# A list scheduler runs sixteen turns instead of eight, and chooses the issued pass by its length plus its stretches of thin TensorE work

## The chip, the cores and the metric

The kernel is one program on one core of one Trainium2 chip. The metric is the device time of one execution in microseconds (us). Before the change the median of 9 runs was 2910.94 us, the lowest 2896.37 and the highest 2915.04.

A core has five instruction queues that matter here: TensorE (PE in the profile, its weight loads under PEld), VectorE (DVE), ScalarE (ACT), GpSimd (POOL) and SyncE (SP, which here only issues DMA transfers). Each engine takes its instructions in the order of its own queue, and engines wait for each other through semaphores. So the kernel's time depends on the order in which instructions stand in these queues.

## What is computed

The reference is a decoder of four layers in float32 on 2048 tokens (32 sequences of 64) of width 256, with a second input `ctx` of 2048 rows of width 128. Every layer is an attention (or state-space) part, a cross-attention to `ctx` and a feed-forward part, each behind a layer norm and added to the residual. With the weights left out of the calls it reads:

```python
x = x + _L0_attn_ref(_layernorm(x), ...)    # attention and gated linear attention, 32 heads
x = x + _L0_xattn_ref(_layernorm(x), ctx_1024, mask, ...)   # cross-attention, 16 heads of 128
x = x + _L0_ffn_ref(_layernorm(x), ...)
x = x + _L1_attn_ref(_layernorm(x), ...)    # state-space mixer, 32 heads, scan over time
x = x + _L1_xattn_ref(_layernorm(x), ctx_1024, ...)
x = x + _L1_ffn_ref(_layernorm(x), ...)     # router, 8 experts of 256
x = x + _L2_attn_ref(_layernorm(x), ...)    # chunked state-space mixer
x = x + _L2_xattn_ref(_layernorm(x), ctx_1024, ...)
x = x + _L2_ffn_ref(_layernorm(x), ...)     # binarized linear layer
x = x + _L3_attn_ref(_layernorm(x), ...)    # attention with fake-quantized fp4 linears
x = x + _L3_xattn_ref(_layernorm(x), ctx_1024, pos, pos, ...)
x = x + _L3_ffn_ref(_layernorm(x), ...)     # top 6 of 64 experts, each at most 128 tokens
```

## The kernel before

The 2048 tokens lie as 16 tiles of 128 tokens, and each tile's residual stays in on-chip memory (`X`, named `__init___x` in the profile). The tiles go through the layers in three groups of 8, 6 and 2 tiles (`GROUPS`, L2559). While one group is in the later layers, the next is recorded beside it in the earlier ones, by `weave` (L2594). Only the last group has nothing behind it: `run_last` (L2585) records its late layers beside the 64 experts of layer 3, which serve the tokens of the first two groups.

Nothing is issued while this is recorded. A `Recorder` keeps each instruction as an `Op` with the engines it may run on, its views of tiles, and the later ops that must follow it (`after`). A copy out of PSUM or an elementwise combination may have two possible engines (`either`, `combine`); on which one it runs, and in which of the buffers of its kind (`Net.SLOTS`, L804) a tile lies, is settled by the scheduler.

The scheduler is `Order` (L539). It goes through planned time: `run` (L621) keeps for each of the five engines the ops whose predecessors are planned, and plans next the one that can start earliest. `duration` (L475) gives the length it assumes for an instruction, and `may_open` (L567) keeps an op from taking a buffer that an earlier op needs. An op may be planned ahead of recorded order by at most `horizon` (120) us of TensorE work. Where TensorE would wait for more than 1.6 us (`IDLE`) and a PSUM bank is free, `fill` (L597) plans a matmul of constants whose result nobody reads, once per step, until the wait is used up. These fillers are named `spare_mm` in the profile.

`in_turns` (L785) repeats this. It plans the program forwards, then plans the reversed graph (`backwards`), with ops numbered by their planned starts (`renumber`), then forwards again, and so on. Each plan starts from the starts of the one before. With `rounds` = 4 there are nine passes, of which the first, third, fifth, seventh and ninth go forwards; these five are the candidates. The one with the least planned length is kept, and `issue` (L2517) writes its instructions to the engines' queues in its order. All instructions carry the line of `issue` in the profile (L2541), so they are told apart by the names of their tiles, where the numbers of layers are left out: `L_block_mm` is `L1_block_mm`.

The names that the prediction's steps use:

- `L_block_mm`, `L_block_b`, `L_block_w` (`unit_L1_block`, L1864): one block of 128 queued tokens of layer 1's experts, whose weights are fetched by the block's expert number. Its output is stored to `result` in device memory by SP.
- `L_result_b` (`unit_L1_result`, L1899): GpSimd gathers these rows back per token by indirect DMA (`DMA_INDIRECT`), two gathers per tile, and VectorE adds them to `X`.
- `cross_scores_mm`, `blocks_b`, `cross_out_mm`: the cross-attention of layers 0 and 1: scores on TensorE, softmax on the other engines, then the product with the context.
- `norm_mm`, `norm_sm`, `pair_mm`, `ssm_heads_mm`: a layer norm with its transposition, and the state-space layers.
- `L_experts_mm`, `L_dense_mm`, `L_parts_b`: layer 3's experts for the first two groups; the same experts, computed densely, for the last group's two tiles; and the sum of the experts' parts at the end of the program.

## Time and profile before

| | |
|---|---|
| median of 9 runs | 2910.94 us |
| the profiled execution | 2918.21 us |
| its span, from the first to the last instruction | 2916.4 us |
| mean granted TensorE clock over the span | 0.972 |
| TensorE instructions | 26626 |
| end of the last matmul, from the span's start | 2887.1 us |
| DMA transfers issued by SP | 665 |

The profile is of a single execution, which took 7.3 us longer than the median. Its views give the busy time of each engine, the busy share in slices of time, the chain of work that ended last, the waits of one engine for another, and the instructions in order of time. A float32 matmul runs as two TensorE instructions, a transposition as one, so a count of TensorE instructions in the profile is larger than in the program. A form such as `32*128` ahead of a matmul's shape is the part of the 128 by 128 array that it uses. "PEclk" is the share of full clock that TensorE was granted in a stretch, and "DMA" the mean busy share of the DMA engines.

### The profile page before, as it was taken

To read this page: it belongs to the slowest core of one execution; us is meant where nothing else is said; L and a number is where in the kernel's file an instruction comes from. 1 tells how busy PE (TensorE), PEld (TensorE's weight loads), DVE (VectorE), ACT (ScalarE), POOL (GpSimd) and SP (SyncE) were. 2 spreads that over 40 slices of the span, in tenths; PEclk is the share of its full clock that TensorE was granted. 3 is DMA by queue.
4 is the path that set the end of the run, shared out by engine and by line. 5 is a ranking of instruction groups with operands and counts; after the bars stand their busy time and mean duration, and the time that the engine had idled before them with its cause. 6 is when DMAs were issued, how large, how long until landed. Compare 5 with 4: busy or idle time off the path is not lost.

```text
span 2916.4 us, 66660 instructions
## 1 busy us (share of the span) xinstructions
PE 2811.5 (96%) x26626; PEld 2342.7 (80%) x26626; DVE 2125.1 (73%) x5139; ACT 1518.7 (52%) x2849; POOL 1522.6 (52%) x1304
## 2 busy tenths in 40 slices
PE   8999999999999999999999999999999999998995
PEld 7888888877878788888888778878797878877674
DVE  5664457775767767867688998787846879988853
ACT  5553226665445454544366656666534665376450
POOL 6762232212666645524554437695615477457665
PEclk8999999999999999999999999999899999999977
DMA  4003320400261146122100110022374122211435
GB/s 179 16 13 116 144 104 19 156 2 31 87 253 46 57 160 206 53 65 64 46 20 27 33 56 17 8 96 81 123 263 171 58 72 83 88 50 59 140 115 175
DMA packets 120313, 259.04 MB, mean 89 GB/s; under 512 B 27077, under 2 KB 81880, under 8 KB 107588
## 3 DMA queue, kind: packets, MB, share of 16 engines
q1 hardware_dynamic: 110212, 230.68, 23.0%
q0 software_dynamic: 9792, 24.10, 2.4%
q8 instruction: 211, 3.46, 0.5%
q14 instruction: 98, 0.80, 0.1%
HBM read 179.38 MB, written 78.77 MB: 89 GB/s over the span
## 4 chain that ended last, share of the span: by engine, by line
PE 80%; DVE 10%; ACT 5%; POOL 2%; issue 2%; DMA 1%; SPq 0%; POOLq 0%; ACTq 0%; DVEq 0%
PE L_xattn_mm L2541 13%; PE ssm_heads_mm L2541 10%; PE pair_mm L2541 10%; PE cross_out_mm L2541 9%; PE L_attn_mm L2541 7%; PE L_ffn_mm L2541 5%; PE L_block_mm L2541 3%; PE turn_mm L2541 3%; PE rope_mm L2541 3%; DVE rope_b L2541 2%; PE L_dense_mm L2541 2%; PE cross_scores_mm L2541 2%; ACT rope_b L2541 2%; PE heads_mm L2541 2%; PE norm_mm L2541 1%
## 5 line engine op out<-in xcount | busy, mean ns | idle before, releaser
L2541 PE MATMUL pair_mm<-norm_b,load_ssm_w 128*128 128x256 f32 x1280 | 307.1, 381 | 1.5 <-DVE __init___x L2541 0.5
L2541 PEld LDWEIGHTS pair_mm<-norm_b,load_ssm_w 128*128 128x128 f32 x1280 | 235.0, 190 | 36.8 <-issue 4.6
L2541 POOL TENSOR_TENSOR L_xattn_sm<-L_xattn_sm,__init___consts 128x8 f32<-128x8 f32 (+2 forms) x64 | 190.4, 2982 | 57.9 <-DVE L_xattn_sm L2541 51.1
L2541 DVE SCALAR_TENSOR_TENSOR ssm_heads_b<-pair_mm,load_ssm_wp,ssm_heads_b 128x252 f32<-128x252 f32 (+2 forms) x480 | 197.2, 467 | 22.5 <-ACT ssm_heads_b L2541 21.3
L2541 ACT COPY rope_b<-rope_mm 32x512 f32<-32x512 f32 x234 | 134.7, 577 | 119.0 <-DVE rope_b L2541 71.4
L2541 POOL TENSOR_TENSOR norm_sm<-norm_sm,__init___consts 128x1 f32<-128x1 f32 (+1 forms) x149 | 93.8, 639 | 168.3 <-DVE norm_sm L2541 151.5
L2541 ACT ACT_TABLE_LOAD x136 | 174.5, 1283 | 10.8 <-DVE L_xattn_sm L2541 2.6
L2541 ACT COPY L_xattn_b<-L_xattn_mm 128x512 f32<-128x512 f32 x177 | 103.8, 591 | 130.8 <-PE L_xattn_mm L2541 127.9
L2541 PE MATMUL rope_mm<-norm_b,load_L_attn_w 128*128 128x128 f32 x1280 | 164.1, 283 | 4.3 <-DVE rope_b L2541 2.7
L2541 PEld LDWEIGHTS rope_mm<-norm_b,load_L_attn_w 128*128 128x128 f32 x1280 | 156.4, 198 | 13.7 <-issue 8.8
L2541 PE MATMUL ssm_heads_mm<-load_ssm_w,ssm_heads_b 128*128 128x256 f32 x640 | 160.0, 384 | 0.2 <-DVE ssm_heads_b L2541 0.2
L2541 ACT ACTIVATE ssm_heads_b<-ssm_heads_b 128x512 f32<-128x512 f32 (+1 forms) x152 | 124.4, 833 | 51.8 <-DVE ssm_heads_b L2541 37.0
L2541 POOL TENSOR_TENSOR ssm_heads_b<-ssm_heads_b,ssm_heads_b 128x1024 f32<-128x1024 f32 x33 | 80.6, 2448 | 135.3 <-DVE ssm_heads_b L2541 116.1
L2541 POOL TENSOR_TENSOR rope_b<-rope_b,__init___consts 128x512 f32<-128x512 f32 x72 | 92.9, 1291 | 81.3 <-DVE rope_b L2541 37.2
L2541 PEld LDWEIGHTS ssm_heads_mm<-load_ssm_w,ssm_heads_b 128*128 128x128 f32 x640 | 116.5, 190 | 23.1 <-issue 9.3
L2541 ACT COPY turn_b<-turn_mm 128x512 f32<-128x512 f32 x194 | 106.4, 602 | 52.2 <-PE turn_mm L2541 51.4
L2541 DVE TENSOR_SCALAR norm_b<-__init___x,norm_sm,norm_sm 128x256 f32<-128x256 f32 x192 | 104.9, 565 | 31.2 <-POOL norm_sm L2541 9.4
L2541 PEld LDWEIGHTS L_xattn_mm<-norm_b,load_L_xattn_w 128*128 128x128 f32 x1024 | 121.1, 192 | 7.8 <-issue 5.9
L2541 ACT COPY norm_b<-norm_mm 128x256 f32<-128x256 f32 (+1 forms) x133 | 56.9, 436 | 134.9 <-PE norm_mm L2541 120.4
L2541 POOL TENSOR_TENSOR heads_b<-heads_b,heads_sm 128x1024 f32<-128x1024 f32 x52 | 101.9, 1967 | 46.6 <-DVE heads_sm L2541 26.0
L2541 PE MATMUL L_xattn_mm<-norm_b,load_L_xattn_w 128*128 128x128 f32 x1024 | 125.4, 276 | 0.0
L2541 PE MATMUL cross_out_mm<-load_L_xattn_w,cross_out_b 128*128 128x256 f32 x512 | 123.4, 390 | 0.3 <-ACT cross_out_b L2541 0.2
(439 smaller groups left out, 7893.6 us busy)
## 6 DMA issues: line engine op xcount, KB each, us to landing
L_block_w<-in_f_rows SPq DMA_DIRECT2D x42, 770.0 KB, 6.5
queue<-far_w SPq DMA_DIRECT2D x14, 1024.0 KB, 10.4
load_ssm_w<-in_s_in SPq DMA_DIRECT2D x12, 1024.0 KB, 6.3
parts<-far_w SPq DMA_DIRECT2D x10, 1024.0 KB, 17.0
slots<-far_w SPq DMA_DIRECT2D x16, 548.0 KB, 7.5
L_experts_b<-slots SPq DMA_DIRECT2D x32, 274.0 KB, 5.2
units_L_xattn_w<-kept_x SPq DMA_DIRECT2D x8, 1024.0 KB, 7.9
L_parts_b<-parts SPq DMA_DIRECT2D x14, 512.0 KB, 7.7
```

What stands on the lines that cost most here:

```text
L2541: done = getattr(getattr(nc, e), method)(*map(real, op.args), **kw)
```

## The change

`in_turns` is called with `rounds` = 8, so that there are seventeen passes and nine candidates. The first five are the candidates of before, since nothing in a pass itself has changed. And the candidate that is issued is no longer that with the least planned length, but that with the least sum of planned length and 3.0 us for each thin stretch. `thin` counts these: planned time is cut into stretches of 3.413 us, each instruction of TensorE adds to the stretch in which it starts a weight (for a matmul, its columns times 1.67 ns times the share of the array that it uses; 0.107 us for a transposition; 0.43 us for a filler), and a stretch with less than 0.36 of its length is thin. `Order.run` notes the starts of fillers for it (`fills`).

```diff
@@ -629,6 +629,7 @@
         stuck, done, oldest, result, self.starts = False, [False] * len(self.ops), 0, [], {}
+        self.fills = []
         while not all(done[oldest:]):
@@ -727,7 +728,9 @@
-            if not filler:
+            if filler:
+                self.fills.append(start)
+            else:
                 done[o.at], self.starts[o] = True, (start, len(result))
@@ -782,14 +785,32 @@
+STRETCH, FULL, THIN = 3.413, 0.36, 3.0
+
+
+def thin(plan):
+
+    work = {}
+    for o, (start, _) in plan.starts.items():
+        if o.ways[0][0] == "tensor":
+            k, m = part(o.ways[0][1], o.args)
+            n = o.args[2].size() * 0.00167 * k * m / P**2 if o.ways[0][1] == "matmul" else 0.107
+            at = int(start / STRETCH)
+            work[at] = work.get(at, 0.0) + n
+    for start in plan.fills:
+        work[int(start / STRETCH)] = work.get(int(start / STRETCH), 0.0) + 0.43
+    return sum(work.get(i, 0.0) < FULL * STRETCH for i in range(max(work)))
+
+
 def in_turns(ops, slots, horizon, spare, rounds):
@@
-        if k % 2 == 0 and (best is None or plan.length < best[0]):
-            best = plan.length, result, {t: t.slot for o, _ in result for t in o.tiles}
+        worth = plan.length + THIN * thin(plan)
+        if k % 2 == 0 and (best is None or worth < best[0]):
+            best = worth, result, {t: t.slot for o, _ in result for t in o.tiles}
@@ -2629,7 +2650,7 @@
-    issue(tc, in_turns(net.nc.ops, Net.SLOTS, 120.0, net.spare, 4), Net.SLOTS)
+    issue(tc, in_turns(net.nc.ops, Net.SLOTS, 120.0, net.spare, 8), Net.SLOTS)
```

The program's work is the same in both kernels. What differs is the order in each queue, the buffers, the choice of engine where there are two, and the number of fillers.

## The prediction, on record before the result was known

> **What bounds the kernel now.** I read the page's busy times first, then its clock row and its chain, then the span in forty equal windows, then the waits of TensorE, and last the order of time around the longest run of fillers.

> ```profile
> PE 2811.5 (96%) x26626; PEld 2342.7 (80%) x26626; DVE 2125.1 (73%) x5139; ACT 1518.7 (52%) x2849; POOL 1522.6 (52%) x1304
> PEclk8999999999999999999999999999899999999977
> PE 80%; DVE 10%; ACT 5%; POOL 2%; issue 2%; DMA 1%; SPq 0%; POOLq 0%; ACTq 0%; DVEq 0%
> ```

> TensorE bounds the kernel: busy for 96% of the span, and 80% of the chain that ended last. Its own work is the same in both kernels, so the change can only move three things: time in which TensorE stands idle (2916.4 - 2811.5 = 104.9 us, of which 29.3 lie behind the last matmul, which ends at 2887.1), time in which it runs on a half-rate clock, and fillers. In the windows, the columns behind the busy times are the granted clock, the DMA share and GB/s:

> ```profile
> 876.00:949.00 73.00, 70.98 (x682) 59.63 (x681) 53.10 (x129) 39.46 (x74) 44.24 (x30) 0.95 0.14 48
> 949.00:1022.00 73.00, 66.03 (x676) 56.64 (x675) 57.72 (x157) 33.16 (x67) 45.23 (x39) 0.98 0.17 55
> 1460.00:1533.00 73.00, 69.18 (x670) 58.43 (x669) 59.55 (x149) 51.20 (x93) 39.96 (x35) 0.95 0.06 20
> 2044.00:2117.00 73.00, 70.19 (x616) 55.94 (x616) 59.21 (x170) 35.93 (x69) 48.59 (x41) 0.86 0.39 126
> 2628.00:2701.00 73.00, 63.86 (x683) 50.64 (x680) 61.58 (x192) 42.69 (x91) 56.95 (x53) 0.91 0.20 64
> 2774.00:2847.00 73.00, 70.42 (x645) 53.43 (x644) 40.13 (x130) 36.22 (x75) 47.75 (x48) 0.79 0.33 113
> ```

> The reader is to see that lost clock and lost busy time sit in few places: near 900 to 1170, near 1500, near 2050 and from 2550 on. Clock lost is (1 - clock) x 73 us. Between 73 and 2628 nine windows are below 1.00 (four at 0.95, four at 0.98, one at 0.86): 14.6 + 5.8 + 10.2 = 30.7 us. The three windows from 2628 to 2847 lose 6.6 + 5.1 + 15.3 = 27.0 us, and the first window, at 0.88, 8.8 us.

> ```profile
> PE L_attn_mm L2541 <- DVE rope_b L2541: 8.3, 5, 2.2
> PE L_ffn_mm L2541 <- DVE L_ffn_sm L2541: 4.0, 2, 2.7
> PE ssm_heads_mm L2541 <- DVE ssm_heads_b L2541: 3.6, 3, 3.1
> ```

> No kind of wait is large (columns: total, times, longest). The idle time is many hand-overs from VectorE and ScalarE of 0.3 to 3.1 us. No single wait can be removed for much; a new order redraws them all.

> **The change, part by part.** *Is another order issued?* Yes. The orders of the two programs differ in nearly every run of rows (TensorE's has 5598 rows before and 5403 after). The order issued before is the fifth candidate; now it is the eighth. With each instruction counted at the median interval of its kind in the rows of before, a TensorE instruction stands 4.1 us of TensorE work from its old place on average (median 3.0, one in a hundred over 17). Stages and their sequence stay; neighbours are shuffled.

> *Engines.* 17 copies out of PSUM move from VectorE to ScalarE (0.59 us on ScalarE, 0.69 on VectorE for 128x512), three small products move the other way, three combinations from VectorE to GpSimd, one of 136 table loads (1.28 us) goes. Spread over 2900 us and on engines busy for 52% to 73%, this is hidden beside TensorE; uncovered it would be a few tenths each. I count 0. SP still issues 665 transfers and GpSimd 204 gathers and scatters.

> *Fillers: 42 before, 35 after.* One filler is two passes; 16 of them took 7.07 us, so 0.44 us each. They mark the places where the planner expects TensorE to stand, so their removal is a gain only where real work takes their place. Sixteen of the 42 stand in one place:

> ```profile
> 2187.32 2.08 PE L2541 MATMUL cross_scores_mm<-contextT_cx,L_xattn_b 128*64 128x64 f32 x64
> 2189.33 4.58 PE L2541 MATMUL L_block_mm<-L_block_w,L_block_b 128*128 128x256 f32 x20
> 2193.76 7.07 PE L2541 MATMUL spare_mm<-__init___consts 128*128 128x256 f32 x32
> 2201.89 4.07 PE L2541 MATMUL cross_out_mm<-blocks_b,context_cx 32*128 32x512 f32 x32 [1.06 <-DVE blocks_b L2541]
> ...
> 2219.81 2.75 PE L2541 MATMUL spare_mm<-__init___consts 128*128 128x256 f32 x12
> 2222.47 1.57 PE L2541 MATMUL norm_mm<-__init___consts,norm_b 128*128 128x128 f32 x8
> ```

> Scores end at 2189.4 and the product with the context starts at 2201.9: a softmax of 12.5 us with 4.4 us of expert blocks beside it, and 8.1 us of fillers and wait. In the new order the scores stand ahead of most blocks: between them and the first `cross_out_mm` are 34 block matmuls of 128x128 (16 passes took 1.95 us in a row near 2178, so 68 take 8.3), 4 of 128x256 (8 passes, 1.8), 8 transpositions (0.9) and two fillers (0.9), 11.9 us. That leaves 0.9 of filler and 0.6 of wait: -6.6 us. The blocks' products on GpSimd now fall among the softmax's, but before its weighting GpSimd idled 3.4 us, which takes them.

> What is late next are the blocks' results. Before: last block matmul done at 2193.9, last store issued by SP at 2196.7, first gather on GpSimd at 2208.3, eight gathers to 2218.5, then the norm's power on the same queue, transpositions at 2222.5: 28.6 us. Now ten gathers stand ahead of that power (two more at 1.25 us), so 31.1 us, against 27.7 us of TensorE work between last block and this `norm_mm` (products with the context, six fillers, 27 matmuls of the third group's `L_ffn_mm`, moved forward). TensorE's queue waits 3.4 us there, with `pair_mm` behind it. The place is worth -3.2 us; bounds -6.6 (results in time) and +2 (they come 5 us later).

> *The other fillers.* Between 2640 and 2726, 16 become 21, thirteen of them in one stand ahead of the last two tiles' `L_attn_mm`: +2.2 us. Three new ones in the first 500 us and one less at 2101: +0.9. Each is bounded by the longest wait in the rows: 3.1 us more or 3.1 less per stand.

> *Half-rate clock.* This is what the added term weighs. Row first: the window from 2044 to 2117 has TensorE busy 70.2 of 73 us and yet a clock of 0.86. The work there is on parts of the array (`64*64`, `8*128`, `32*128`), and no wait ahead of the last matmul is over 3.1 us. [...] The nine windows with loss between 73 and 2628 lose 30.7 / 9 = 3.4 us each. How many go, nothing shows: bounds are all nine gone (-30.7) and as many new ones (+30.7). The issued pass is now weighed by them at all, and it displaced the old one, which still is a candidate, so I take two fewer, an estimate: -6.8 us.

> *The end.* Behind the last matmul lie 29.3 us of `L_parts_b` sums. In both orders the last of them is loaded behind the stores of the last two tiles and followed by the same short chain on VectorE and GpSimd: 0 (bounds 2 us either way).

> *Sum:* -3.2 + 2.2 + 0.9 - 6.8 = -6.9 us. The profiled execution of 2918.2 us would become 2911.3; it stood 7.3 above the median, so the median becomes 2904. All other hand-overs are redrawn too: 75.6 us of idle time ahead of the last matmul plus 66.5 of clock. If some forty places of 2 us are redrawn independently, their sum moves by about 2 x sqrt(2 x 40) = 18 us; many are forced by data and stay, so I take two thirds, 12 us.

> **The rivals.** *No change.* The last 260 us are the serial chain of the last two tiles, with VectorE at 18.45 of 20 us between 2640 and 2660 and the lowest clock. If the eighth candidate brings two more half-rate losses there (3.4 each), they pay for the two gone earlier: -6.9 + 6.8, 2911. For it: the end has five more fillers. Against it: these keep TensorE's array full while it waits.

> *Slower, through the gathers.* The gathers are behind the last store, and that shares its queue with 1024 KB weight loads, which took 6.3 to 17.0 us to land. If the first gather starts 17.0 instead of 11.6 us after the last store, TensorE waits 5.4 us more, and a stand of 8.8 us brings a half-rate stretch (3.4); without the gain in thin stretches: -3.2 + 5.4 + 3.4 + 2.2 + 0.9 = +8.7, 2920. It decides from about 2.5 us later than before. For it: a 1024 KB load of `units_L_xattn_w` that was issued 20 us after the last store now stands just ahead of it. Against it: before, three such loads stood there too.

> *Nothing is changed*, because the old pass wins again: the orders exclude it.

> **How the numbers follow.** Forecast (a gain of some us) 46%, its own range 2892 to 2905. No change 20%: within 0.2% (5.8 us, about what a measurement of this kernel can tell from no change), 2905 to 2917. Slower 34%: the gathers, or the redrawn hand-overs coming out badly, which the 12 us allow. Two tenths left out, 2904 with 1.6 times 12 us each way: 2884 to 2924.

> **What would show it.** Right: few fillers near 2190 and `cross_out_mm` less than 2 us after the block matmuls; a mean clock above 0.972, with the window near 2050 above 0.86. Wrong: a wait of over 6 us at `norm_mm` behind `L_result_b`; clock lost in windows that had 1.00; or VectorE's hand-overs from 2550 on grown by ten us or more. The prediction fails most easily where it estimates: in the number of thin stretches, and in the redrawing.

## The result: slower by 1.2%, most of it clock

The changed kernel takes 2945.14 us (median of 15 runs, 2936.3 to 2952.0), the kernel before 2911.78 us (46 runs, 2896.37 to 2924.14): ratio 1.0118, 95% interval 1.0103 to 1.0132, some 33 us. The forecast was 2904, the range 2884 to 2924.

The page after, in the parts that were shown of before (busy times, clock row, chain):

```profile
PE 2819.7 (96%) x26612; PEld 2353.5 (80%) x26612; DVE 2127.6 (72%) x5122; ACT 1518.7 (52%) x2862; POOL 1543.9 (52%) x1307
PEclk8999999999999999999999999999999999999987
PE 76%; DVE 12%; ACT 5%; issue 3%; POOL 3%; DMA 1%; SPq 0%; DVEq 0%; POOLq 0%; ACTq 0%
```

TensorE issues 14 instructions fewer, the fillers that are gone, and yet is busy 8.2 us longer. The other engines are as busy as before, but for 21 us on GpSimd. In the chain TensorE's share falls from 80% to 76%, and VectorE's, GpSimd's and "issue" rise by a point or two each. So neither more work nor a new bottleneck shows here; the same work takes longer.

The windows of after, with the clock behind the busy times:

```profile
584.00:657.00 73.00, 72.03 (x614) 58.47 (x613) 50.10 (x132) 42.95 (x63) 9.37 (x7) 0.95 0.00 1
876.00:949.00 73.00, 69.50 (x661) 56.66 (x654) 44.70 (x110) 34.62 (x67) 38.04 (x27) 0.91 0.17 60
1460.00:1533.00 73.00, 72.03 (x694) 60.96 (x693) 65.24 (x173) 52.28 (x97) 47.00 (x43) 1.00 0.05 17
1825.00:1898.00 73.00, 69.69 (x716) 53.88 (x718) 54.13 (x107) 39.09 (x79) 49.64 (x41) 0.88 0.03 7
2044.00:2117.00 73.00, 67.72 (x613) 56.08 (x612) 64.74 (x164) 34.92 (x69) 55.52 (x48) 0.91 0.36 123
2774.00:2847.00 73.00, 69.34 (x1030) 54.15 (x1018) 58.00 (x210) 48.36 (x106) 47.35 (x49) 0.91 0.49 150
```

Read each against its twin of before, four of which stand in the prediction; the other two are:

```profile
584.00:657.00 73.00, 72.56 (x656) 57.70 (x656) 55.16 (x147) 44.35 (x70) 12.96 (x9) 1.00 0.01 2
1825.00:1898.00 73.00, 70.83 (x791) 57.49 (x790) 58.77 (x147) 46.84 (x91) 48.15 (x41) 1.00 0.04 8
```

The places near 1500 and 2050 that the prediction hoped to mend are mended (0.95 to 1.00, 0.86 to 0.91), and so is the window from 2774 (0.79 to 0.91). But windows that had 1.00 before now lose clock: 584 to 657 (0.95) and 1825 to 1898 (0.88). Set side by side, lost clock seems merely to have moved.

The waits of TensorE (total, times, longest) tell the same story:

```profile
PE turn_mm L2562 <- ACT heads_b L2562: 6.5, 3, 3.8
PE L_attn_mm L2562 <- DVE L_attn_b L2562: 6.4, 3, 3.2
PE L_block_mm L2562 <- DVE L_block_b L2562: 5.1, 4, 2.3
```

Other pairs lead the list than before, and none is large. When the same instructions of the two traces are set against each other, after's lag (the median over the instructions within 25 us) is 13 us by 650, 15 by 1450, back at 3 to 9 from 1500 to 1800, 20 by 1950, 24 by 2450, 34 at 2700 and 24 at 2850: many steps, both ways.

### Where the 33 us are

Two accounts were made. The first goes by the traces up to the last matmul. "Clock" is half of the time at half rate (a granted clock of 0.50; passes of a filler follow each other by 0.216 us at full rate, and by 0.427 in the half-rate stretch of after at 2736.9) in which TensorE worked; "fillers" are their passes at 0.216 us; the rest is TensorE's own work. Both kernels were profiled a second time, under the names `c_before_again` and `c_after_again`:

| execution | last matmul, us from the first | idle | clock | fillers | own work | half-rate stretches |
|---|---|---|---|---|---|---|
| before | 2885.9 | 74.4 | 67.2 | 18.1 | 2726.1 | 19 |
| before, again | 2864.4 | 79.5 | 38.8 | 18.1 | 2728.0 | 13 |
| after | 2910.6 | 90.9 | 77.9 | 15.1 | 2726.7 | 29 |
| after, again | 2909.7 | 93.8 | 76.2 | 15.1 | 2724.5 | 29 |

TensorE's own work agrees within 3.5 us in all four. By the means of each pair, after stands idle 15 us more, loses 24 us more to the clock and spends 3 us less on fillers. From the first execution of each alone, one would have read +16.5 idle and +10.7 clock, and called waits the larger part. That profile of before caught an execution with much half rate: by span and clock it lost 82.9 us, the second one 52.1. The runs of before reach from 55 to 82, so the two stand at its ends, and their mean is near the runs' mean of 67.2 below.

The second account needs no trace. Every run lists its span and mean granted clock, so span x (1 - clock) is the time lost to the clock and span x clock the rest. On one chip, number 12 in the records of the runs:

| kernel | runs | lost to the clock, us | the rest, us |
|---|---|---|---|
| before | 17 | 67.2 | 2840.3 |
| after | 6 | 97.6 | 2846.3 |

The 17 executions of after behind the result, whose chip is not on record, give 97.7 and 2846.1. The clock takes 30 us more, the rest 6 us more. (This counts clock lost while TensorE has nothing to do, too, as in the 25.9 us at half rate behind the last matmul of before: among the runs of before, 1 us lost goes with 0.8 us of span, so by an estimate the 30 are worth about 25.) Both accounts name the clock as the larger part.

### One of the new places

Near 1850 both orders run the cross-attention of small heads. First before, in order of time:

```profile
1860.80 0.61 PE L2541 MATMUL L_xattn_mm<-norm_b,load_L_xattn_w 128*128 128x128 f32 x4
1861.34 2.98 PE L2541 MATMUL heads_mm<-values_b,turn_b 128*64 128x18 f32 x96
1864.25 1.09 PE L2541 MATMUL turn_mm<-__init___consts,heads_b 128*128 128x128 f32 x8
```

Then after:

```profile
1856.30 1.15 PE L2562 MATMUL cross_scores_mm<-L_xattn_b,L_xattn_b 128*64 128x64 f32 x32 [1.35 <-DVE turn_b L2562]
1858.22 1.37 PE L2562 MATMUL turn_mm<-__init___consts,heads_b 128*128 128x128 f32 x8 [0.77 <-ACT keys_apart_b L2562]
1860.14 4.27 PE L2562 MATMUL small_scores_mm<-keys_apart_b,keys_apart_b 32*64 32x256 f32 x32 [0.56 <-DVE heads_sm L2562]
1864.35 5.31 PE L2562 MATMUL heads_mm<-values_b,turn_b 128*64 128x18 f32 x96
```

The clock of the ten microseconds from 1860, before and then after:

```profile
1860.00:1870.00 10.00, 10.00 (x181) 9.48 (x179) 8.18 (x16) 6.68 (x13) 8.99 (x7) 1.00 0.04 10
```

```profile
1860.00:1870.00 10.00, 9.68 (x130) 7.45 (x131) 7.66 (x14) 6.86 (x11) 7.60 (x4) 0.64 0.01 2
```

Before, 96 passes of `heads_mm` (a `128*64` part of the array, 18 columns each) take 2.98 us between products on the full array. After, three waits of 0.6 to 1.4 us come first, and then two thin products stand back to back; the 96 passes take 5.31 us, and 32 passes of `small_scores_mm` take 4.27, which took 1.44 us seven microseconds earlier. The three waits sum to 2.7 us. Half rate begins at 1862.71 only, so the 4.27 us are two things: 24 of the 32 passes start by 1862.12, at full clock, with stands of 0.5 us within them and 0.4 us behind them that the line doesn't show as waits, and the last 1.6 us lie at half rate. The half-rate stretch ends at 1872.95. It is 10.24 us long at a granted clock of 0.50 and costs half of that, 5.1 us, of which 5.31 - 2.98 = 2.3 us are the 96 passes. The second execution of after has a half-rate stretch of 13.7 us at the same place, and the second of before has none there, so it belongs to the order.

### The profile page after: what moved, and what is told of

Read it like the earlier page. It is cut to its first block, busy times and chain, and to the rows that moved or that the text cites. A ratio compares the mean times of both kernels' runs of the same rounds, so it can differ in the third digit from the quotient of the medians.

```text
span 2940.8 us, 66641 instructions
## 1 busy us (share of the span) xinstructions
PE 2819.7 (96%) x26612; PEld 2353.5 (80%) x26612; DVE 2127.6 (72%) x5122; ACT 1518.7 (52%) x2862; POOL 1543.9 (52%) x1307
## 4 chain that ended last, share of the span: by engine, by line
PE 76%; DVE 12%; ACT 5%; issue 3%; POOL 3%; DMA 1%; SPq 0%; DVEq 0%; POOLq 0%; ACTq 0%
PE L_xattn_mm L2562 12%; PE ssm_heads_mm L2562 10%; PE pair_mm L2562 9%; PE cross_out_mm L2562 9%; PE L_attn_mm L2562 7%; PE L_ffn_mm L2562 4%; PE turn_mm L2562 3%; PE rope_mm L2562 2%; PE L_block_mm L2562 2%; PE heads_mm L2562 2%; ACT rope_b L2562 2%; PE L_dense_mm L2562 2%; DVE rope_b L2562 2%; PE cross_scores_mm L2562 2%; PE small_scores_mm L2562 2%
## 5 line engine op out<-in xcount | busy, mean ns | idle before, releaser
L2562 DVE SCALAR_TENSOR_TENSOR ssm_heads_b<-pair_mm,load_ssm_wp,ssm_heads_b 128x252 f32<-128x252 f32 (+2 forms) x480 | 196.2, 467 | 19.2 <-ACT ssm_heads_b L2562 18.1
L2562 POOL TENSOR_TENSOR norm_sm<-norm_sm,__init___consts 128x1 f32<-128x1 f32 (+1 forms) x149 | 93.8, 635 | 172.3 <-DVE norm_sm L2562 157.6
L2562 ACT COPY L_xattn_b<-L_xattn_mm 128x512 f32<-128x512 f32 x167 | 97.5, 587 | 164.5 <-PE L_xattn_mm L2562 152.9
L2562 POOL TENSOR_TENSOR ssm_heads_b<-ssm_heads_b,ssm_heads_b 128x1024 f32<-128x1024 f32 x36 | 87.4, 2428 | 158.2 <-DVE ssm_heads_b L2562 108.2
L2562 POOL TENSOR_TENSOR rope_b<-rope_b,__init___consts 128x512 f32<-128x512 f32 x76 | 102.2, 1346 | 81.0 <-ACT rope_b L2562 51.9
L2562 ACT ACTIVATE ssm_heads_b<-ssm_heads_b 128x1024 f32<-128x1024 f32 (+1 forms) x152 | 124.0, 832 | 37.9 <-DVE ssm_heads_b L2562 16.5
L2562 PE MATMUL L_attn_mm<-load_L_attn_w,L_attn_b 128*128 128x256 f32 x512 | 125.0, 388 | 0.0
L2562 PEld LDWEIGHTS L_xattn_mm<-norm_b,units_L_xattn_w 128*128 128x128 f32 x1024 | 119.8, 192 | 4.3 <-issue 2.3
```

What stands on the lines that cost most here:

```text
L2562: done = getattr(getattr(nc, e), method)(*map(real, op.args), **kw)
```

## The experiments

Eighteen runs follow. The letters in the expectations stand for these theories. A: any redrawn order scatters around a mean, and the fifth candidate, the kernel before, was a good draw. B: more turns pack the plan tighter and leave less room for what the planner doesn't know. C: the planner's own length tells the time. D: its durations for VectorE and GpSimd are too short, and truer ones help. E: the loss is in the choice of engine. T: the planned count of thin stretches tells the real clock. K and W: fillers in waits spare clock, or only trade one loss for another.

By the numbers in the records, chip 12 ran e1 to e4 and the c and n kernels, and chip 11 ran f5 and f6; on both, before takes 2910 to 2911 us, as it does in the result. The other runs came to three other chips (0, 6 and 13), on which before itself takes 3008 to 3011 us; only ratios are compared across chips.

### Other candidates of the same planner

The new length of the search without the new term issues the ninth candidate:

```diff
-    issue(tc, in_turns(net.nc.ops, Net.SLOTS, 120.0, net.spare, 4), Net.SLOTS)
+    issue(tc, in_turns(net.nc.ops, Net.SLOTS, 120.0, net.spare, 8), Net.SLOTS)
```

> Sixteen turns, but the candidate with the least planned length is issued, as before the change: this is the ninth candidate, which the planner puts ahead of all others in length. Theory A (redrawn hand-overs: a candidate's time on the chip scatters by about 1% around a mean that its planned figures do not tell, and the fifth was a low draw): somewhere in 2915 to 2950 us, not the fastest of the candidates. Theory B (each further turn packs the plan closer, with less room at the hand-overs, and costs time on the chip): the slowest of the candidates, 2945 to 2960. Theory C (length tells the time, and the new weighing for thin stretches spoiled the choice): faster than before the change, 2895 to 2908.

Measured: 2924.69 against 2911.38 us, ratio 1.0046 (1.0029 to 1.0064).

The sixth and the seventh candidate are issued by keeping the last pass of five and of six rounds:

```diff
-        if k % 2 == 0 and (best is None or plan.length < best[0]):
+        if k == 2 * rounds:
...
-    issue(tc, in_turns(net.nc.ops, Net.SLOTS, 120.0, net.spare, 4), Net.SLOTS)
+    issue(tc, in_turns(net.nc.ops, Net.SLOTS, 120.0, net.spare, 5), Net.SLOTS)
```

> The sixth candidate is issued, one forward pass after the one issued before the change. By the planner's length it is the worst of the fifth to ninth. Theory A: 2915 to 2950, its place among the candidates not that of its planned length. Theory B: a little slower than the fifth and faster than the seventh, near 2920. Theory C: the slowest of the five, over 2925.

Measured: 2941.26 us, 1.0106 (1.0081 to 1.0131).

> The seventh candidate is issued. By the planner's length it lies just behind the eighth, and far ahead of the sixth. Theory A: 2915 to 2950, no order by planned length. Theory B: between the sixth and the eighth, near 2932. Theory C: faster than the sixth by 6 us or more, and close to the fifth.

Measured: 2922.98 us, 1.0037 (1.0017 to 1.0058).

So the sixth to the ninth candidate stand at 1.0106, 1.0037, 1.0118 and 1.0046: all slower than the fifth, and in no order with the number of turns. B falls. C falls as well: the ninth is the shortest plan and not the fastest. By the planner's own figures and the account of the runs' clocks, all on chip 12:

| candidate | planned length, us | planned thin stretches | lost to the clock, us | the rest, us | ratio |
|---|---|---|---|---|---|
| fifth (before) | 2683.6 | 9 | 69.2 | 2841.5 | 1 |
| sixth | 2691.9 | 11 | 88.2 | 2852.1 | 1.0106 |
| seventh | 2685.7 | 10 | 81.1 | 2840.8 | 1.0037 |
| eighth (after) | 2683.9 | 8 | 97.6 | 2846.3 | 1.0118 |
| ninth | 2678.8 | 10 | 85.9 | 2836.8 | 1.0046 |

By the new score (length plus 3.0 us for each thin stretch) the eighth stands 2.7 us ahead of the fifth and 0.9 ahead of the ninth: against the fifth, a single thin stretch decided the choice.

The new term chose the candidate with the fewest planned thin stretches, and that one loses the most clock of all. The ninth is 5 us better than before in everything but the clock, and loses 17 us there.

### The old engines in the new order

Between the two kernels 643 operations run on another engine (246 from VectorE to ScalarE, 232 back, 84 from VectorE to GpSimd, 81 back). This kernel keeps after's order and buffers, with before's engine for each operation:

```diff
+        if k == 8:
+            old = dict(result)
...
-    return best[1]
+    return [(o, old.get(o, e)) for o, e in best[1]]
```

> The changed kernel's order of all instructions and its buffers, but every instruction that may run on two engines runs on the one that it had before the change (17 copies go back from ScalarE to VectorE, larger products from GpSimd to VectorE). Theory E (the choice of engines costs the time: GpSimd has 21 us more work, 1543.9 against 1522.6, and VectorE's instructions get slower beside it): at least half of the 33 us comes back, 2925 or less. Theory A (the order costs it): the time stays within 10 us of the changed kernel, 2935 to 2955, or is worse, since the order was made for the other engines.

Measured: 3007.47 us, 1.0323 (1.0296 to 1.0350). Its longest waits of TensorE:

```profile
PE turned_mm L2564 <- POOL L_xattn_b L2564: 8.7, 6, 3.8
PE turn_mm L2564 <- ACT heads_b L2564: 7.6, 4, 3.8
PE ssm_heads_mm L2564 <- DVE ssm_heads_b L2564: 7.4, 6, 2.7
```

Putting the engines back costs 62 us more. TensorE now waits for GpSimd and VectorE where the plan had spread the work otherwise; 119 us are lost to the clock. Order and engines are one plan and can't be judged apart in this way. E finds no support. That a VectorE instruction can be slow beside GpSimd the trace of after shows: at 390.92 us a 128x256 scaling into `norm_b` takes 3.69 us beside a 128x2048 product of 3.61 us on GpSimd, where the median of the 192 such scalings is 0.41. What this costs in the new order stays untested.

### Other durations and horizons

The planner was given longer durations for VectorE and GpSimd, nearer to the measured ones, with eight turns and no thin term, and with sixteen and the term:

```diff
-            return 0.16 + n * 0.00052 + 0.11 * small
+            return 0.2 + n * 0.00052 + 0.23 * small
...
-        return 0.15 + n * 0.00104 + 0.06 * small
+        return 0.19 + n * 0.00104 + 0.06 * small
...
-    return 0.14 + n * (0.00174 if full < 2 else 0.0022)
+    return 0.14 + n * (0.00174 if full < 2 and n != 512 else 0.0022)
```

> The kernel before the change, eight turns and choice by length, with the planner's durations for VectorE and GpSimd raised to what the trace of before shows (VectorE 0.04 us more for each instruction and 0.12 more where a small operand goes with a large one in on-chip memory, GpSimd's 512-column products at 1.27 instead of 1.03 us). Theory D (the plan goes wrong on the chip because it has VectorE too fast: 2248 us planned against 2433 measured, so hand-overs that it counts as covered are not): fewer and shorter waits, idle time before the last matmul down from 74 by 20 us or more, time 2880 to 2900. Theory A (any new plan is a new draw, and the draws scatter by 1%): anything from 2900 to 2950.

Measured: 3020.75 against 3007.89 us, 1.0040 (1.0023 to 1.0057).

> The changed kernel, sixteen turns and the choice with thin stretches, with the same raised durations. The planner now counts 14 thin stretches in the candidate that it issues (the seventh) against 22 in the one that the run with eight turns and the same durations issues, at nearly equal planned length. Theory T (the term for thin stretches is right, and it failed only since the planner's times were too short to see the stretches): at least 10 us faster than the run with raised durations and eight turns, and fewer half-rate stretches. Theory A: no relation to that run, within 20 us of it on either side.

Measured: 3065.37 us, 1.0197 (1.0151 to 1.0244).

And the horizon of 120 us was changed by one microsecond each way, which alters nothing but which orders the passes find:

```diff
-    issue(tc, in_turns(net.nc.ops, Net.SLOTS, 120.0, net.spare, 4), Net.SLOTS)
+    issue(tc, in_turns(net.nc.ops, Net.SLOTS, 119.0, net.spare, 4), Net.SLOTS)
```

> The kernel before the change with a horizon of 119 instead of 120 us, which means nothing by itself and gives another family of plans; all of its candidates have a planned length that is longer by about 0.7% than the one issued before. Theory A: 2910 to 2950, a draw like the others. Theory C (planned length tells the time): 2925 to 2940. A time at or below 2911 speaks against both.

Measured: 3015.10 us, 1.0031 (1.0015 to 1.0047).

> The kernel before the change with a horizon of 121 instead of 120 us. Its issued candidate has a planned length that is longer by about 0.6% than the one issued before, and the fewest thin stretches in the planner's count of all plans seen (5, where the kernel before the change has 9 and the changed one 8). Theory T (few planned thin stretches mean few half-rate stretches on the chip): under 15 half-rate stretches and a clock over 0.976, time below 2920. Theory A: 18 to 30 half-rate stretches, 2910 to 2950.

Measured: 3025.67 us, 1.0070 (1.0042 to 1.0097).

D falls: truer durations made the plan no better. T falls for a second time: the plan with a horizon of 121 counts 5 thin stretches, the fewest of all, and loses 127.8 us to the clock, where before with its count of 9 lost 127.7 on that chip; g1's count was 22 and g2's 14, and g2 takes 45 us longer than g1 and loses no less to the clock (148.6 us in four runs that spread from 134 to 163, against 139.5). A holds as far as it goes: all eight other plans, from 1.003 to 1.020, are slower than that of before, and the eighth candidate is not outside their scatter.

### Fillers added, by a rule that was too coarse

Fillers were put ahead of 43 waits of TensorE in before and 48 in after, in any PSUM bank that the order left alone for its next 60 steps (place: number):

```diff
+FILLS = {
+    134: 3, 208: 5, 228: 1, 323: 5, 564: 3, 1120: 5, 1267: 2, 6876: 4, 7161: 2, 7384: 2,
...
+def padded(order, place, spare):
...
-    return best[1]
+    return padded(best[1], place, spare)
```

> The kernel before the change, its order and buffers untouched, with more fillers: 103 filler matmuls are put ahead of the 43 TensorE instructions that had waited for over 0.6 us in the profile of before, as many as fit into each wait. Theory K (half-rate stretches come from windows in which TensorE has too little work, and a wait filled with work on the whole array prevents them): the clock's loss before the last matmul, 67 us, falls by 20 us or more, the fillers lie in time that was idle, and the time falls by 10 to 25 us, 2886 to 2901. Theory W (the clock's loss comes from the work on small parts of the array, not from the waits, or the waits move when they are filled): clock unchanged within 0.003, time 2911 to 2925.

Measured: 3014.44 against 3008.19 us, 1.0028 (1.0011 to 1.0044).

> The changed kernel, its order and buffers untouched, with 144 fillers ahead of the 48 TensorE instructions that had waited for over 0.6 us in its own profile. It has 29 half-rate stretches before the last matmul where before had 19, and 78 us of loss through them where before had 67. Theory K: more is won than in the kernel before, 15 to 35 us, 2910 to 2930, and what remains against the filled kernel before is the difference in waits. Theory W: 2940 to 2960.

Measured: 3036.37 us, 1.0089 (1.0059 to 1.0118).

This could not tell K from W, since most places had no free bank: only 11 further fillers ran in f1 and 21 in f2. Some of them waited for a bank themselves, as f1's waits show (the first line is of another kind, and is met again below):

```profile
PE L_experts_mm L2581 <- issue: 12.0, 24, 1.1
...
PE spare_mm L2581 <- DVE rope_b L2581: 3.7, 1, 3.7
...
PE spare_mm L2581 <- DVE L_attn_b L2581: 3.3, 1, 3.3
```

### Fillers added only where a bank was free

By each kernel's own trace, 15 waits of before and 20 of after had a bank that had been free since before the wait began. They got 36 and 60 fillers (place: number, bank):

```diff
+FILLS = {
+    134: (3, 7), 7161: (2, 0), 7387: (1, 4), 7482: (1, 4), 7860: (2, 5), 11272: (7, 7), 16168: (1, 1), 16666: (3, 6),
+    21392: (2, 0), 22195: (2, 6), 22516: (1, 0), 22601: (2, 7), 22651: (5, 4), 23677: (3, 3), 23682: (1, 5),
+}
...
-    return best[1]
+    return padded(best[1], place, spare)
```

> The kernel before with 36 further filler products, put only ahead of the 15 waits of TensorE for which, by its own trace, a PSUM bank of the filler's kind had been free since before the wait began. Every planned step, engine and buffer is otherwise that of the kernel before. Theory K (idle stretches thin the work, thin work halves the clock, so filling them spares clock): the fillers take the place of waits, the half-rate stretches fall from 19 to 15 or fewer, the clock's cost from 67 us to about 55, and the time falls by 5 to 12 us. Theory W (filling only trades one loss for another: the fillers delay what follows the wait, and other stretches become thin): half-rate stretches 17 or more, time within 0.2% or longer by up to 10 us.

Measured: 2993.92 against 3010.66 us, 0.9940 (0.9924 to 0.9957), faster than the kernel before on that chip. (The counts of stretches in the expectation are those of the first profile of before; here the kernel shows 26.)

> The changed kernel with 60 further filler products, put by the same rule ahead of 20 of its waits. Theory K: half-rate stretches fall from 29 to 23 or fewer, the clock's cost from 78 us to about 60, and the time falls by 8 to 18 us, so that a third to a half of the change's loss is undone without touching the order. Theory W: half-rate stretches 26 or more, the time within 0.2% of the changed kernel's (ratio to before near 1.012) or above it.

Measured: 3025.54 us, 1.0051 (1.0034 to 1.0068).

The changed kernel itself had not been run on that chip, so 1.0051 could not be set against its 1.0118. The two kernels unedited ran on chip 12, and f3's kernel once more, beside one with only the 36, on chip 11:

> The kernel before, unedited, profiled on this chip so that the others of this group have a profile of their own chip beside them. Ratio to itself 1.000; if this chip is the slower one again (before near 3010 us), its waits for the issue of instructions and its clock's cost (above 67 us) show here too.

> The changed kernel, unedited, on the chip of this group. Theory K says that the further fillers (1.0051 with 60 of them) undid part of the loss: then the changed kernel alone stays at 1.009 to 1.014. Theory W says they did nothing: then it is at 1.003 to 1.008 on this chip.

> The kernel before with its own 42 fillers and 36 more ahead of the 15 waits with a free bank, once more, now beside the next kernel on one chip. Theory K (fillers spare the clock where they take the place of a real wait): ratio 0.990 to 0.997 again. Chance of one chip alone: 0.998 to 1.003.

```diff
-    return padded(best[1], place, spare)
+    return padded([(o, e) for o, e in best[1] if o.at >= 0], place, spare)
```

> The kernel before with only the 36 fillers that the trace placed, and without the planner's own 42. Leaving out the planner's made no difference (1.001), so if the trace's fillers alone carry the gain the ratio stands at 0.990 to 0.997, like the kernel with both. If a gain comes only from both together, it stands at 0.998 to 1.004.

Measured: before in one execution 2896.70; after 2945.06, 1.0123 (1.0097 to 1.0149); f6, the same kernel as f3, 2907.20 against 2910.94, 0.9987 (0.9965 to 1.0009); f5 2914.89, 1.0025 (1.0007 to 1.0044). The gain of 0.6% is thus not found on chip 11. What the 60 fillers did to after on f4's chip stays open, since after alone never ran there.

### Fillers taken away

The fillers that the planner itself put in are left out; nothing of the result depends on them:

```diff
-    return best[1]
+    return [(o, e) for o, e in best[1] if o.at >= 0]
```

> The kernel before with its 42 own filler products left out and nothing else altered (84 passes of 0.216 us, 18.1 us of TensorE). Theory K: the places that they filled turn thin, half-rate stretches rise by five or more, and the time is 0 to 20 us longer, although 18 us of work are gone. Theory W: the clock's cost stays and the time falls by 5 to 18 us.

> The changed kernel with its 35 own filler products left out (15.1 us of TensorE). Theory K: half-rate stretches rise by five or more above its own, time 0 to 20 us longer than the changed kernel's. Theory W: the clock's cost stays, time falls by 5 to 15 us. If the two kernels without fillers stand closer than the two with them, the fillers' three us and part of the clock's eleven belong to the fillers that the new pass doesn't have.

Measured: 2910.56 against 2910.25 us, 1.0010 (0.9990 to 1.0031), and 2948.22 us, 1.0126 (1.0093 to 1.0159): no difference to the kernels with fillers. The clocks of the runs say why:

| kernel | further fillers | chip | lost to the clock, against before's | the rest, against before's |
|---|---|---|---|---|
| n_nofill_before | -42 | 12 | +11.7 | -8.8 |
| f5_only_free | -42, +36 | 11 | +8.3 | -1.9 |
| f6_free_again | +36 | 11 | -12.1 | +7.7 |
| f3_free_before | +36 | 13 | -24.8 | +8.9 |
| f4_free_after (has the change too) | +60 | 13 | -5.1 | +20.3 |

Mean spans and clocks of two profiled executions, without fillers and with 36 more:

```profile
core 0: 2914.1 us, clock 0.972
```

```profile
core 0: 2906.7 us, clock 0.980
```

K's mechanism is shown, in both directions and for the kernel after too (lost 109.8 us without fillers, 97.6 with): work put into waits spares clock. W's outcome holds on chips 11 and 12 all the same, because the fillers cost nearly what the clock gives back (8.8 us for 11.7, 7.7 for 12.1). On chip 13 the clock gives back 24.8 us for 8.9. Why more there isn't settled. Nor do the effects add: -42 and +36 alone come to -0.4 us of clock, and f5 with both loses 8.3 more than before.

## Why the prediction was wrong

**What bounds the kernel: right.** TensorE's own work is the same, 2724 to 2728 us in four executions, and all of the difference is idle time, clock and fillers, as the prediction set out.

**Which order is issued: right.** *Engines at 0:* only net counts were given (17, three, three), where 643 operations had changed engine. What these cost by themselves stays open.

**The place at 2190: right in its sum, by luck.** After, in order of time:

```profile
2196.26 2.09 PE L2562 MATMUL cross_scores_mm<-contextT_cx,L_xattn_b 128*64 128x64 f32 x64
2198.28 0.70 PE L2562 MATMUL spare_mm<-__init___consts 128*128 128x256 f32 x2
...
2205.06 1.10 PE L2562 MATMUL L_block_mm<-L_block_w,L_block_b 128*128 128x256 f32 x4 [1.08 <-DVE L_block_b L2562]
...
2212.40 1.10 PE L2562 MATMUL L_block_mm<-L_block_w,L_block_b 128*128 128x256 f32 x4 [1.08 <-DVE L_block_b L2562]
2213.55 2.00 PE L2562 MATMUL cross_out_mm<-blocks_b,context_cx 32*128 32x512 f32 x16
2216.58 2.00 PE L2562 MATMUL cross_out_mm<-blocks_b,context_cx 32*128 32x512 f32 x16 [1.03 <-DVE blocks_b L2562]
...
2235.02 2.75 PE L2562 MATMUL spare_mm<-__init___consts 128*128 128x256 f32 x12
2237.85 0.76 PE L2562 MATMUL norm_mm<-__init___consts,norm_b 128*128 128x128 f32 x4
```

`cross_out_mm` starts right behind the blocks. Of sixteen fillers two are left (the other stands at 2209.7). Fillers and waits of the place were 7.07 + 1.06 + 2.75 = 10.9 us and are now 0.70 + 0.60 + 2.75 of fillers and 0.29 + 1.08 + 1.08 + 1.03 of waits, 7.5 us: -3.4, where -3.2 was forecast. But the forecast was -6.6 for fillers and wait, and +3.4 for a wait at `norm_mm` for the gathers. The first came out at half its size, since hand-overs of the blocks and of the softmax (1.08, 1.08 and 1.03 us) took its place; the second did not come at all, for no wait shows at this `norm_mm` and none over 0.7 us up to 2262. The two errors cancel. The rival by the gathers is wrong in its mechanism too, though its sign came true.

**The other fillers: right** (27 outside this place against 20, 7 x 0.43 = 3.0 us; 3.1 was forecast). **The end at 0: right** (29.3 and 29.0 us behind the last matmul).

**The half-rate clock: the step that failed.** It was forecast at -6.8 us, "two fewer, an estimate"; the traces show +24 us and the runs' clocks +30. Two things were wrong with it. The estimate leaned on the change's own count: a pass "weighed by them" should have fewer. That count falls by one only, from 9 to 8, where the half-rate stretches of the traces rise from 19 and 13 to 29 and 29. The candidates and the horizons show that this count doesn't order the real losses at all. And the rows that it started from were one execution's: the windows from 2628 on, which lost 27.0 us there, are not the kernel's own. Of the second execution of before, the window from 2774, which stood at 0.79:

```profile
2774.00:2847.00 73.00, 70.17 (x656) 55.22 (x646) 38.45 (x116) 30.52 (x62) 48.63 (x49) 0.98 0.46 169
```

Counted as "clock" is in the first account, the loss from 2550 on was 29.3 us in one execution of before and 10.9 in the other (24.1 and 21.0 after). Between 500 and 2000 the kernels keep apart in all four: 14.9 and 10.2 before, 29.4 and 29.5 after. Of the 24 us more, 17 are lost there.

**The redrawn hand-overs: off in size and placed at zero.** Idle time grew by 15 us, 2.4 of them at the place near 2190, against a band of 12 either way that was centred on 0. The centre was the error: the kernel before is not an average plan but the fastest of the nine that were measured, and a redrawing of a good draw is more likely to be worse. The prediction's own check, VectorE's hand-overs from 2550 on, didn't show it: idle time there grew by 2 us only. It grew most between 2000 and 2550 (7.4 and 9.0 us before, 18.5 and 18.2 after).

**The checks named beforehand.** "A mean clock above 0.972" failed (0.968 in both executions). "The window near 2050 above 0.86" came true with 0.91, and meant nothing: before has 0.93 there in its second execution. "Clock lost in windows that had 1.00" came true, and was the right sign to look for.

**The standing to the median.** That the profile stood 7.3 us above the median was taken as an offset to subtract. It was clock: the profiled execution had 0.972, as low as the lowest of 17 later runs of before on chip 12, which reach 0.981 and whose spans follow their clock with a correlation of -0.94.

**What stays open:** why the fifth candidate has fewer thin windows on the chip between 500 and 2000 than the eighth, though the planner counts nearly the same for both (chance is consistent with all runs, and not shown), and what contention between engines adds.

## What to carry to other kernels

Where a planner's candidates differ by less than its model errs, a longer search or a further term in the score is another draw and not an improvement; the kernel in hand may be a good draw already, and then a redrawing is likely to lose, here 0.3% to 2.0% in eight of eight. Before a term is added to a planner's score, compare its count with traces of several orders that exist already: the count of thin stretches would have failed that test. And when time varies from run to run, take span and clock of all runs before reading one profile's losses as the kernel's own.

## What the runs showed of the hardware

| weight | before | after | all 20 traces of this study |
|---|---|---|---|
| under 0.36 | 17 of 25 | 27 of 36 | 483 of 615 |
| 0.36 to 0.42 | 2 of 14 | 2 of 15 | 39 of 310 |
| above | 0 of 765 | 0 of 753 | 2 of 15222 |

Idle time alone doesn't tell them: of the 524 windows ahead of half rate in all 20 traces, TensorE was idle for less than 1 us in 157, and for more than 3.3 us in 7 (in before and after, in 19 and in none of 48). Near 1860 in after, the windows from 1852.5 on weigh 0.40, 0.47 and 0.23, and the one behind the 0.23 is the first at half rate. In the window of 0.23 TensorE is busy for 2.67 of 3.41 us, much of it on a part of the array. A stand without any work has half rate behind it too: in before the last matmul ends at 2887.1 us, and from 2890.49 the clock is 0.50 to the end of the span. So the threshold of `thin` fits the traces. What it lacks is the real time: it counts 9 and 8 in the plans, where the first traces have 25 and 36 such windows at full rate.

**Clock lost differs between executions of one program.** The kernel before lost between 55 and 82 us to the clock in 17 runs on chip 12, with the rest of its span between runs spread by 2.8 us (one standard deviation). Small shifts against the grid, and the fifth of the thin windows that pass (132 of 615), may decide it; this is not shown by itself.

**Chips differ.** On three other chips before takes 3008 to 3011 us: by the runs' clocks 125 to 128 us are lost to the clock there (66 to 69 on chips 11 and 12) and 2878 to 2883 spent on the rest (2840 to 2842). The traces from there show waits that the profile can put down only to the issue of instructions, such as the 24 waits of `L_experts_mm` shown for f1; in both traces of before the same group shows none. What makes them is not known from these runs.
